# Scores of layer 1 for pairs of heads, in halves of 64 queries, two products side by side in TensorE's columns

## The chip, the cores and the metric

The kernel runs on one core of a Trainium2 chip. The metric is the device time of one execution in microseconds (us), the median of three runs: 2057.37 us before the change (2057.35 to 2057.42). Inside a core, several engines run at the same time and wait for each other through semaphores: TensorE (PE in the profile; its weight loads are shown apart as PEld), VectorE (DVE), ScalarE (ACT), GpSimd (POOL), and SyncE (SP), which only starts transfers.

## The reference

Two transformer layers on x of shape (4, 512, 512). What matters here is the attention of layer 1: 32 query heads and 8 key heads of 128, over 512 tokens, causal, in f32.

```python
q = (hidden_states @ w_q).reshape(B, S, Hkv, g, D)     # 8 key heads, 4 query heads each
k = (hidden_states @ w_k).reshape(B, S, Hkv, D)
v = (hidden_states @ w_v).reshape(B, S, Hkv, D)
scores = jnp.einsum('bqhgd,bkhd->bhgqk', q, k) * scale
causal = jnp.tril(jnp.ones((S, S), dtype=bool))
scores = jnp.where(causal, scores, -jnp.inf)
probs = jax.nn.softmax(scores.astype(jnp.float32), axis=-1).astype(q.dtype)
attn = jnp.einsum('bhgqk,bkhd->bqhgd', probs, v)
return attn.reshape(B, S, Hq * D) @ w_o
```

So the scores of one head are 512 x 512, of which only the lower triangle counts. Query i sees keys 0 to i.

## The kernel before

The whole program is one hand-ordered sequence: each engine executes its instructions in the order in which the code issues them. Layer 0 takes about the first 190 us, the attention of layer 1 runs from there to about 1750 us, and the feed-forward part of layer 1 fills the rest.

The attention of layer 1 is cut into 32 blocks (batch times key head), each with 4 query heads; `score(s, i)` counts the heads through, s = 4n + h. Two heads, a pair, make one `window` (L1120). Window w issues the scores and softmax of pair w+1 and the value products of pair w, and in between it deals out `fill`: the pieces of the q, k, v and output projections (`seven`, L738), each a quarter product of 256 or 128 columns into one of three banks of PSUM from the pool `ps_sc`, and gathered from there by DVE or ACT.

Inside a window the eight score tiles of the pair, `(s, i)` with i the tile of 128 queries, go through a short software pipeline, one step per slot: in slot j the score of tile j (`score`, L872), the division of tile j-1 (`divide`, L889), and the 32 by 32 transposes of tile j-2 (`flip`, L895). The tiles come in the order i = 3, 2, 1, 0 for the first head and then 3, 2, 1, 0 for the second (L1125). In slots 8 and 9 the value products of the pair before follow (`value`, L920), and at the end `carry` (L911) sends the flipped probabilities through transfers that complete the transpose.

For one tile, `score` does this: one product of 128 queries with the first 128(i+1) keys into a bank taken in turn from `ps_mm` and `ps_tr` (L878), an addition of a 128 by 128 mask to the last, diagonal block (L879; the mask holds 0 or -3e38), a maximum over the row (L881), and the exponential with its sum on ACT (L883). The product is f32, and one such product is two instructions of TensorE with a weight load each; the queries are the stationary operand (128 columns of the array), the keys the moving one.

`value` collects a head's output in `av` and copies it on ACT into `oT[n][:, h, :]` (L933). From `oT` POOL makes the left sums of the output projection (`sums_o`, L760), and `o_pieces` (L837) uses them.

The modulation of each layer, in `M` (L386), is of use below as a measuring point: four f32 products of 32 output columns each, placed at columns 0, 32, 64 and 96 of the array (L390).

Of the kernel before, what the change touches and what calls it, by code (L numbers as in the profile page):

```python
# [8 lines left out]
F32 = mybir.dt.float32  # L9
# [4 lines left out]
ALU = mybir.AluOpType  # L14
# [3 lines left out]
P = 128  # L18
# [6 lines left out]
HKV, G, D1 = 8, 4, 128  # L25
INTER = 1792
FB = 256
EPS = 1e-5
NEG = -3.0e38
EXACT = 4096.0  # L30


@with_exitstack
def adaln_two_layers(ctx: ExitStack, tc: tile.TileContext, a, out: bass.AP):
    nc = tc.nc
# [9 lines left out]
    conste = early.enter_context(tc.tile_pool(name="conste", bufs=1))  # L45
    lnp = early.enter_context(tc.tile_pool(name="ln", bufs=1))
    gap = early.enter_context(tc.tile_pool(name="gate_a", bufs=B))
    ps_mm = early.enter_context(tc.tile_pool(name="ps_mm", bufs=2, space=PSUM))
    ps_sc = early.enter_context(tc.tile_pool(name="ps_sc", bufs=3, space=PSUM))
    ps_tr = early.enter_context(tc.tile_pool(name="ps_tr", bufs=2, space=PSUM))  # L50
# [83 lines left out]
    with tc.using_default_side("right"):  # L134
# [15 lines left out]
    nc.vector.memset(mhalf, -0.5)  # L150
    ident = const.tile([P, P], F32, name="ident")
    make_identity(nc, ident)
    mask = conste.tile([P, P], F32, name="mask")
    nc.gpsimd.memset(mask, 0.0)
    nc.gpsimd.affine_select(
        out=mask, in_=mask, compare_op=ALU.is_ge, fill=NEG, base=0,
        pattern=[[-1, P]], channel_multiplier=1,
    )

    o_sb = [l0w.tile([P, NT, 32], F32, name=f"o{b}") for b in range(B)]  # L160
    for b in range(B):
# [3 lines left out]
        cid, pattern=[[0, 1]], base=0, channel_multiplier=1,  # L165
# [54 lines left out]
    ADD, SUB = ALU.add, ALU.subtract  # L220
# [5 lines left out]
    def left_sums(eng, t, s):  # L226

        A11, A21, A12, A22 = quarters(t)
        S3, S2, S4 = s[:, 0], s[:, 1], s[:, 2]
        eng.tensor_tensor(S3, A11, A21, SUB)  # L230
        eng.tensor_tensor(A21, A21, A22, ADD)
        eng.tensor_tensor(S2, A21, A11, SUB)
        eng.tensor_tensor(S4, A12, S2, SUB)
        return {1: A11, 2: A12, 3: S4, 4: A22, 5: A21, 6: S2, 7: S3}
# [15 lines left out]
    def sums_in(kind, n):  # L250
        w = weights[kind, n]
        s = T["wp"].tile([P, 3, 2, w.shape[2] // 2], F32, tag=f"s{kind}", name=f"s{kind}")
        left[kind, n] = left_sums(nc.gpsimd, w, s)
# [455 lines left out]
    for o in order:  # L709
        name, _, eng = o.partition("/")  # L710
# [24 lines left out]
    def bank(shape, name):  # L735
        return ps_sc.tile(shape, F32, tag="sc", name=name)
# [18 lines left out]
    qT, kT, vs, oT, prob = {}, {}, {}, {}, {}  # L755
# [8 lines left out]
    def sums_h(b, engs):  # L764
        s = hp.tile([P, 4, 2, HALF], F32, tag="hT", name="hsum")
        right["h", b] = right_sums(engs, h1[b], [s[:, i] for i in range(3)], s[:, 3])
# [40 lines left out]
    def q_pieces(n):  # L807
        def start():
            for j in range(2):
                qT[n, j] = at.tile([P, 2, S], F32, tag="qT", name="qT", bufs=3)  # L810
            return corners(qT[n, 0], qT[n, 1])

        return seven(lambda: left["q", n], lambda: right["h", n // HKV], gather(start), SEVENTH)
# [37 lines left out]
    BK = 32  # L851
    NG = P // BK
# [13 lines left out]
    def blocks(s, i):  # L866

        if s // 2 == LAST:
            return plain[:, s % 2, i, : (i + 1) * P].rearrange("p (j q) -> p j q", q=BK)
        return prob2[s // 2 % 2][:, : NG * (i + 1), s % 2, i, :]  # L870

    def score(s, i):  # L872
        n, h = divmod(s, G)
        w = (i + 1) * P
        pool, tag = ((ps_mm, "mm"), (ps_tr, "tr"))[i % 2]
        ps = pool.tile([P, 512], F32, tag=tag, name="sc")
        q = qT[n, h // 2][:, h % 2, :]
        nc.tensor.matmul(ps[:, :w], q[:, i * P : w], kT[n][:, :w], start=True, stop=True)  # L878
        nc.vector.tensor_tensor(ps[:, i * P : w], ps[:, i * P : w], mask, ADD)  # L879
        nmx = small.tile([P, 1], F32, tag="nmx", name="nmx")  # L880
        nc.vector.tensor_reduce(nmx, ps[:, :w], AX.X, ALU.max, negate=True)  # L881
        den = small.tile([P, 1], F32, tag="den", name="den")
        nc.scalar.activation(  # L883
            blocks(s, i), ps[:, :w].rearrange("p (j q) -> p j q", q=BK),
            AF.Exp, bias=nmx, accum_out=den,
        )
        prob[s, i] = den

    def divide(s, i):  # L889
        p = blocks(s, i)  # L890
        rden = small.tile([P, 1], F32, tag="rden", name="rden")
        nc.vector.reciprocal(rden, prob.pop((s, i)))  # L892
        nc.scalar.mul(p, p, rden)  # L893
# [17 lines left out]
    def carry(pair):  # L911

        for a_ in range(NG):
            src = prob2[pair % 2][a_ * BK : (a_ + 1) * BK]
            src = src.rearrange("r (k j) h i q -> r j k (h i q)", j=NG)
            for j in range(NG):
                dst = turned[j * BK : (j + 1) * BK, :, a_]
                nc.sync.dma_start(dst, src[:, j])

    def value(s):  # L920

        n, h = divmod(s, G)
        if h == 0:
            oT[n] = at.tile([P, G, S], F32, tag="oT", name="oT")
        av = bank([P, 512], "av") if s % 2 else ps_av.tile([P, 512], F32, tag="av", name="av")
        pT = straight if s // 2 == LAST else turned
        for k in range(NT):
            nc.tensor.matmul(  # L928
                av.rearrange("p (a n) -> p a n", a=NG)[:, :, BK * k :], vs[n][:, k, :],
                pT[:, k, :, P * (s % 2) + BK * k : P * (s % 2 + 1)],  # L930
                start=(k == 0), stop=(k == NT - 1),
            )
        nc.scalar.copy(  # L933
            oT[n][:, h, :].rearrange("p (i a q) -> p a i q", a=NG, q=BK),
            av.rearrange("p (a i q) -> p a i q", a=NG, q=BK),
        )


    def scan(i):
# [122 lines left out]
    def decide():  # L1062
        size = small.tile([P, 1], F32, tag="size", name="size", bufs=1)
        nc.vector.tensor_reduce(size, sizes, AX.X, ALU.max)
        nc.vector.tensor_scalar(size, size, EXACT, None, ALU.is_gt)
        return size
# [9 lines left out]
    def split_pieces(got):  # L1076

        def piece(c):
            if c == 0:
                h2[0] = [hp.tile([P, KC, S], F32R, tag="hT", name=f"h2_{i}") for i in range(2)]  # L1080
            pt, m = bank([P, S], "lnT"), modT[1]
            for t in range(NT):
                nc.tensor.transpose(
                    pt[:, t * P : (t + 1) * P], got["xn"][:, t, c * P : (c + 1) * P], ident
                )

            tag, bufs = (("v", 4), ("kT", 3))[c % 2]
            tm = at.tile([P, E], F32, tag=tag, name="tm", bufs=bufs)
            nc.scalar.activation(
                tm, pt, AF.Identity, bias=m[:, 2, c, 0:1], scale=m[:, 3, c, 0:1]  # L1090
            )
            hi, lo = (h[:, c, :] for h in h2[0])
            nc.scalar.copy(hi, tm)

            lows.append(lambda: nc.vector.tensor_tensor(lo, tm, hi.bitcast(F32), SUB))

        lows = []
        return [lambda c=c: piece(c) for c in range(KC)], [lambda c=c: lows[c]() for c in range(KC)]
# [17 lines left out]
    def run(*fill):  # L1116
        for f in fill:
            f()

    def window(w, fill, side=(), late=(), values=(8, 9)):  # L1120


        fill, side = list(fill), list(side)
        more = w + 1 <= LAST
        tiles = [(2 * w + 2 + h, i) for h in range(2) for i in (3, 2, 1, 0)]  # L1125

        lag, turn_ = (5, turn) if w + 1 == LAST else (2, flip)
        slots = lag + 7
        share = [len(fill) // slots + (i < len(fill) % slots) for i in range(slots)]
        each = -(-len(side) // slots)  # L1130
        for i in range(slots + 1):
            if more and i >= lag:
                turn_(*tiles[i - lag])
            if more and 0 < i < 9:
                divide(*tiles[i - 1])
            if more and i < 8:
                score(*tiles[i])
            for h in range(2):
                if w >= 0 and values[h] == i:
                    value(2 * w + h)  # L1140
            if i < slots:
                for _ in range(share[i]):
                    fill.pop(0)()
                for _ in range(each):
                    if side:
                        side.pop(0)()
        run(*late)
        if w + 1 < LAST:
            carry(w + 1)
# [5 lines left out]
    run(*put(2, x[2]))  # L1155
    sums_h(0, (nc.gpsimd, nc.vector))
    nc.gpsimd.memset(prob2[0], 0.0)
    sums_in("k", 0)
    sums_in("v", 0)
    sums_wo(0)  # L1160
# [9 lines left out]
    run(*put(3, x[3]), *put(0, x[0]), *put(1, x[1]))  # L1170
    q = q_pieces(1)
    window(-1, v_pieces(0))
    load("v", 1)
    pending = []
    begun = []

    for n in range(NBLK):
        b, g = divmod(n, HKV)
        ahead, behind = n + 1 < NBLK, n > 0
        if n > 0:  # L1180
            q = q_pieces(n + 1) if ahead else []
# [3 lines left out]
        kind, m = "vk"[n % 2], n // 2 + n % 2  # L1185
# [40 lines left out]
        else:  # L1226
            first_weights()
            t, r = split_pieces(got)
# [5 lines left out]
            s = at.tile([P, 3, 2, HALF], F32, tag="soT", name="soT", bufs=1)  # L1234
# [262 lines left out]
```

## Time and profile before

The profiled execution took 2058.11 us, of which its span, from the first to the last instruction, is 2056.2 us. The rest lies around the span.

| what | value |
|---|---|
| median of the runs | 2057.37 us |
| profiled execution / span | 2058.11 / 2056.2 us |
| score products L878, duration of one pass of 512, 384, 256, 128 columns | 593, 487, 379, 274 ns |
| weight load of 128 columns for L878 | 191 ns |
| mask on DVE, L879 | 284 ns, 512 times |
| maximum on DVE, L881, 512 / 384 / 256 columns | 692 / 558 / 425 ns |
| exponential on ACT, L883, 512 / 384 / 256 columns | 687 / 581 / 474 ns |
| output copy on ACT, L933 | 581 ns, 128 times |

How to read it: a line of a group names the source line, engine, operation, the tiles written and read, the shapes and how often; then the busy time in us and the mean duration of one in ns; then how long the engine was idle just before and what ended that. In a timeline each row has the start in us, the time in us, the engine, and the instructions merged into the row. A pass of TensorE is shown from its start to the modelled end of its pipeline, so passes in a row overlap in the view; how fast they stream is read from the distance between starts.

### The profile page before, as it was taken

What the parts mean: (1) busy time and instruction counts of PE and PEld (TensorE: products, weight loads), DVE (VectorE), ACT (ScalarE), POOL (GpSimd) and SP (SyncE); (2) the same over time, 40 slices, a digit from 0 to 9 for tenths busy, and PEclk for the clock granted to TensorE, in tenths of its full rate; (3) what the DMA queues carried; (4) which work ended last, traced back from release to release, by engine and by line L of the source; (5) the groups of instructions that cost most, each with busy time, mean ns of one, the idle gap of its engine ahead of it and who ended that gap; (6) DMA issues with size and microseconds to landing.
All of it is one profiled execution on the core that took longest, in us unless ns stands there. A gap on an engine that the chain in (4) does not pass through costs nothing.

```text
span 2056.2 us, 27492 instructions
## 1 busy us (share of the span) xinstructions
PE 2020.9 (98%) x9219; PEld 1580.4 (77%) x9219; DVE 1362.9 (66%) x3323; ACT 878.9 (43%) x1998; POOL 756.9 (37%) x656
## 2 busy tenths in 40 slices
PE   6999999999999999999999999999999999999998
PEld 4655777878787887877787878787877777888887
DVE  6766776677667666766677676667666674655554
ACT  3421554445444444544444445444444454223322
POOL 2314234434336443353473334337333333800000
PEclk8799999999999999999999999999999999999999
DMA  8310656676657766655766665567656556600000
GB/s 299 123 62 30 173 151 175 159 175 153 144 144 192 180 160 161 164 144 152 186 182 163 154 164 133 144 154 177 167 144 154 141 128 202 196 21 1 21 21 22
DMA packets 243640, 288.59 MB, mean 140 GB/s; under 512 B 23250, under 2 KB 184018, under 8 KB 243492
## 3 DMA queue, kind: packets, MB, share of 16 engines
q1 hardware_dynamic: 242964, 285.71, 52.8%
q8 instruction: 76, 1.25, 0.3%
q10 hardware_dynamic: 528, 1.05, 0.2%
q14 instruction: 72, 0.59, 0.1%
HBM read 142.99 MB, written 11.57 MB: 75 GB/s over the span
## 4 chain that ended last, share of the span: by engine, by line
PE 94%; DVE 3%; ACT 1%; issue 1%; DMA 1%; POOL 0%; SPq 0%; DVEq 0%; ACTq 0%
PE quarter L746 46%; PE av L928 14%; PE sc L878 13%; PE p_gate L1347 5%; PE p_up L1347 5%; PE acc L1366 4%; PE ffn L634 2%; PE lnT L477 1%; PE modps L390 1%; PE lg L593 1%; PE qkv_ps L507 1%; PE modT_ps L403 1%; PE add_ps L578 1%; DVE bnst L60 0%; DMA c_sb<-in_L_cT_dram 0%
## 5 line engine op out<-in xcount | busy, mean ns | idle before, releaser
L878 PE MATMUL sc<-kT,qT 128*128 128x512 f32 (+3 forms) x1024 | 355.1, 433 | 0.0
L928 PE MATMUL av<-x,v 128*128 128x512 f32 x1008 | 295.7, 437 | 3.7 <-DMA x<-p 3.7
L928 PEld LDWEIGHTS av<-x,v 128*128 128x128 f32 x1008 | 190.3, 192 | 110.7 <-issue 66.5
L881 DVE TENSOR_REDUCE nmx<-sc 128x1 f32<-128x512 f32 (+3 forms) x512 | 251.6, 491 | 17.7
L893 ACT ACTIVATE x<-x,rden 128x512 f32<-128x512 f32 (+3 forms) x256 | 143.6, 561 | 235.4 <-DVE rden L892 235.4
L778 DVE TENSOR_TENSOR qT<-qT,quarter 128x512 f32<-128x512 f32 x224 | 150.5, 684 | 133.9 <-PE quarter L746 127.7
L893 ACT ACTIVATE p<-p,rden 128x512 f32<-128x512 f32 (+3 forms) x256 | 143.7, 561 | 221.5 <-DVE rden L892 219.8
L879 DVE TENSOR_TENSOR sc<-sc,mask 128x128 f32<-128x128 f32 x512 | 145.5, 284 | 136.5 <-PE sc L878 135.6
L842 DVE TENSOR_TENSOR acc<-acc,quarter 128x512 f32<-128x512 f32 x196 | 134.5, 686 | 134.6 <-PE quarter L746 134.4
L230 POOL TENSOR_TENSOR sq<-wq 128x512 f32<-128x512 f32 x32 | 40.6, 1269 | 471.5 <-DMA wq<-in_L_attn_w_q_dram 453.0
L878 PEld LDWEIGHTS sc<-kT,qT 128*128 128x128 f32 x1024 | 182.6, 191 | 24.2
L746 PEld LDWEIGHTS quarter<-wo,oT 128*128 128x128 f32 x744 | 140.9, 190 | 43.9 <-issue 20.1
L746 PE MATMUL quarter<-wo,oT 128*128 128x256 f32 x744 | 171.1, 379 | 0.2 <-ACT oT L933 0.2
L883 ACT ACTIVATE p<-sc,nmx 128x512 f32<-128x512 f32 (+3 forms) x256 | 135.1, 528 | 75.8 <-DVE nmx L881 67.1
L883 ACT ACTIVATE x<-sc,nmx 128x512 f32<-128x512 f32 (+3 forms) x256 | 134.9, 527 | 70.1 <-DVE nmx L881 65.4
L933 ACT COPY oT<-av 128x512 f32<-128x512 f32 x128 | 74.3, 581 | 167.0 <-PE av L928 165.0
L896 DVE STREAM_TRANSPOSE p<-p 128x512 f32<-128x512 f32 (+3 forms) x256 | 129.4, 506 | 2.0 <-ACT p L893 0.5
L896 DVE STREAM_TRANSPOSE x<-x 128x512 f32<-128x512 f32 x248 | 125.0, 504 | 1.3 <-ACT x L893 0.9
L746 PE MATMUL quarter<-hsum,sq 128*128 128x256 f32 x512 | 121.1, 379 | 1.4 <-DVE hsum L244 1.4
L746 PEld LDWEIGHTS quarter<-hT,wq 128*128 128x128 f32 x512 | 97.2, 190 | 32.4 <-issue 14.8
L746 PE MATMUL quarter<-hsum,wq 128*128 128x256 f32 x512 | 121.0, 379 | 0.0
L746 PE MATMUL quarter<-hT,wq 128*128 128x256 f32 x512 | 120.9, 379 | 0.0
(257 smaller groups left out, 3752.7 us busy)
## 6 DMA issues: line engine op xcount, KB each, us to landing
x<-p SPq DMA_DIRECT2D x512, 128.0 KB, 3.7
x<-x SPq DMA_DIRECT2D x496, 128.0 KB, 3.8
wq<-in_L_attn_w_q_dram SPq DMA_DIRECT2D x32, 1024.0 KB, 5.6
wo<-in_L_attn_w_o_dram SPq DMA_DIRECT2D x31, 1024.0 KB, 5.7
wm<-in_L_wmod_dram SPq DMA_DIRECT2D x12, 1024.0 KB, 9.6
wk<-in_L_attn_w_k_dram SPq DMA_DIRECT2D x16, 512.0 KB, 3.7
wv<-in_L_attn_w_v_dram SPq DMA_DIRECT2D x16, 512.0 KB, 3.8
xn<-x_d SPq DMA_DIRECT2D x28, 256.0 KB, 5.9
```

The costliest lines, as they stand in the source:

```text
L746: nc.tensor.matmul(ps[:, m, :], l[:, k, m * P : (m + 1) * P], r[:, k, :], start=(k == 0), stop=(k == 1),)
L778: nc.vector.tensor_tensor(c[out], c[v], ps, ADD if sign > 0 else SUB)
L842: nc.vector.tensor_tensor(osum[:, i - 1], osum[:, i - 1], ps, ADD)
L878: nc.tensor.matmul(ps[:, :w], q[:, i * P : w], kT[n][:, :w], start=True, stop=True)
L879: nc.vector.tensor_tensor(ps[:, i * P : w], ps[:, i * P : w], mask, ADD)
L881: nc.vector.tensor_reduce(nmx, ps[:, :w], AX.X, ALU.max, negate=True)
L883: nc.scalar.activation(blocks(s, i), ps[:, :w].rearrange("p (j q) -> p j q", q=BK), AF.Exp, bias=nmx, accum_out=den,)
L893: nc.scalar.mul(p, p, rden)
L896: nc.vector.transpose(blocks(s, i), blocks(s, i))
L928: nc.tensor.matmul(av.rearrange("p (a n) -> p a n", a=NG)[:, :, BK * k :], vs[n][:, k, :], pT[:, k, :, P * (s % 2) + BK * k : P * (s % 2 + ...
L1347: nc.tensor.matmul(ps[kind], w[kind][:, k, c * P : (c + 1) * P], h2[b % 2][i][:, k, :], start=(k == 0 and i == 0), stop=(k == KC - 1 and i ...
L1366: nc.tensor.matmul(acc[t], act[i][:, t * P : (t + 1) * P], w[:, c, :], start=(n == 0 and i == 0), stop=(n == NI - 1 and i == 1),)
```

## The change

A pair's scores for tile i are now issued together, by the first head's `score`, as four products of 64 queries each: first half and second half of the 128 queries, for each of the two heads. The first half leaves out the last 64 keys, which lie above the diagonal for all its queries. Two products of the same half, one for each head, go to the two 64-column halves of the array and so to the two halves of the partitions of two different banks. For the first head the first half of the queries lies in partitions 0 to 63; for the second head it lies in partitions 64 to 127, with the halves exchanged.

What follows from that: there are two masks, the second with its halves exchanged; the mask is applied by a minimum, so that what stands in the columns that are no longer computed is covered too; four fixed banks `sc_ps` from `ps_mm` and `ps_tr` replace the tiles taken in turn, and are set to 0 once; the tiles of a window come in the order i = 3, 2, 1, 0 with both heads of each i in succession; and the second head's output copy becomes two copies, which put the exchanged halves back.

```diff
+TOP = 3.4028234e38
...
-    mask = conste.tile([P, P], F32, name="mask")
-    nc.gpsimd.memset(mask, 0.0)
-    nc.gpsimd.affine_select(
-        out=mask, in_=mask, compare_op=ALU.is_ge, fill=NEG, base=0,
-        pattern=[[-1, P]], channel_multiplier=1,
-    )
+    masks = conste.tile([P, 2, P], F32, name="masks")
+    nc.gpsimd.memset(masks, TOP)
+    HP = P // 2
+    for m, ps_, first_ in ((0, slice(0, P), 0), (1, slice(0, HP), HP), (1, slice(HP, P), 0)):
+        nc.gpsimd.affine_select(
+            out=masks[ps_, m], in_=masks[ps_, m], compare_op=ALU.is_ge, fill=NEG, base=first_,
+            pattern=[[-1, P]], channel_multiplier=1,
+        )
...
+    sc_ps = [[p.tile([P, 512], F32, tag=t, name="sc") for _ in range(2)] for p, t in ((ps_mm, "mm"), (ps_tr, "tr"))]
+
+    def product(s, i):
+        n, h = divmod(s, G)
+        for half in range(2):
+            w = i * P + HP * (half + 1)
+            for h_ in range(2):
+                q = qT[n, (h + h_) // 2][:, (h + h_) % 2, :]
+                at_ = HP * (half ^ h_)
+                nc.tensor.matmul(
+                    sc_ps[h_][i % 2][at_ : at_ + HP, :w], q[:, w - HP : w], kT[n][:, :w],
+                    start=True, stop=True, tile_position=(0, at_),
+                )
+
     def score(s, i):
-        n, h = divmod(s, G)
-        w = (i + 1) * P
-        pool, tag = ((ps_mm, "mm"), (ps_tr, "tr"))[i % 2]
-        ps = pool.tile([P, 512], F32, tag=tag, name="sc")
-        q = qT[n, h // 2][:, h % 2, :]
-        nc.tensor.matmul(ps[:, :w], q[:, i * P : w], kT[n][:, :w], start=True, stop=True)
-        nc.vector.tensor_tensor(ps[:, i * P : w], ps[:, i * P : w], mask, ADD)
+        if s % 2 == 0:
+            product(s, i)
+        w, ps = (i + 1) * P, sc_ps[s % 2][i % 2]
+
+        nc.vector.tensor_tensor(ps[:, i * P : w], ps[:, i * P : w], masks[:, s % 2], ALU.min)
...
-        nc.scalar.copy(
-            oT[n][:, h, :].rearrange("p (i a q) -> p a i q", a=NG, q=BK),
-            av.rearrange("p (a i q) -> p a i q", a=NG, q=BK),
-        )
+        dst = oT[n][:, h, :].rearrange("p (i a q) -> p a i q", a=NG, q=BK)
+        src = av.rearrange("p (a i q) -> p a i q", a=NG, q=BK)
+        if h % 2 == 0:
+            nc.scalar.copy(dst, src)
+        else:
+            nc.scalar.copy(dst[:, 2:], src[:, :2])
+            nc.scalar.copy(dst[:, :2], src[:, 2:])
...
-        tiles = [(2 * w + 2 + h, i) for h in range(2) for i in (3, 2, 1, 0)]
+        tiles = [(2 * w + 2 + h, i) for i in (3, 2, 1, 0) for h in range(2)]
...
     nc.gpsimd.memset(prob2[0], 0.0)
+    for ps in sc_ps[0] + sc_ps[1]:
+        nc.vector.memset(ps, 0.0)
```

## The prediction

> **What bounds the kernel now.** I read the page from the top: busy times, the chain that ended last, then who waited on TensorE.
>
> ```profile
> span 2056.2 us, 27492 instructions
> PE 2020.9 (98%) x9219; PEld 1580.4 (77%) x9219; DVE 1362.9 (66%) x3323; ACT 878.9 (43%) x1998; POOL 756.9 (37%) x656
> ...
> PE 94%; DVE 3%; ACT 1%; issue 1%; DMA 1%; POOL 0%; SPq 0%; DVEq 0%; ACTq 0%
> PE quarter L746 46%; PE av L928 14%; PE sc L878 13%; PE p_gate L1347 5%; PE p_up L1347 5%; PE acc L1366 4%; PE ffn L634 2%; PE lnT L477 1%; PE modps L390 1%; PE lg L593 1%; PE qkv_ps L507 1%; PE modT_ps L403 1%; PE add_ps L578 1%; DVE bnst L60 0%; DMA c_sb<-in_L_cT_dram 0%
> ```
>
> TensorE is the chain, and the scores (L878) are 13% of it. The list of waits, for PE alone, says that nothing in the attention holds TensorE up:
>
> ```profile
> PE modps L390 <- DMA wm<-in_L_wmod_dram: 11.9, 1, 11.9
> PE modT_ps L403 <- DVE part L286: 4.3, 3, 2.0
> PE av L928 <- DMA x<-p: 3.7, 1, 3.7
> ```
>
> So a nanosecond more or less of TensorE time in the attention is a nanosecond of the end. The groups by form show the score products that are to change, and the one f32 product of the kernel that already runs in column tiles (modps, four tiles of 32 columns):
>
> ```profile
> L878 PE MATMUL sc<-kT,qT 128*128 128x512 f32 x256 | 130.9, 593 | 0.0
> L878 PE MATMUL sc<-kT,qT 128*128 128x384 f32 x256 | 103.6, 487 | 0.0
> L878 PE MATMUL sc<-kT,qT 128*128 128x256 f32 x256 | 76.2, 379 | 0.0
> L878 PE MATMUL sc<-kT,qT 128*128 128x128 f32 x256 | 49.3, 274 | 0.0
> ```
>
> Each f32 product is two instructions (x256 for 128 products). A duration holds the pipeline's latency too; throughput is the distance between starts. In the timeline of PE at 809 us, 14 passes of 256 columns take 3.19 us; less one latency-bearing pass of 0.38, that is 2.81/13 = 0.216 us for a pass, 0.84 ns a column, 1.68 ns a column for both passes. Check: 64 pairs of heads x 2 x (128+256+384+512) columns x 1.68 ns = 275 us, against 12.9% of 2056 = 265 us in the chain.
>
> **What the skill says, and whether the trace agrees.** "TensorEngine Tiling (Array Packing)", Key Properties, says that changing the tiling mode, not just the tile, drains TensorE, and that different tiles run in parallel. "TensorE: Matmul & The Clock Gate", Part 3, gives 2.38x for three column tiles of 512 columns. The trace has both, in f32, in the PE timeline around one modps group:
>
> ```profile
> 34.21 0.93 PE L477 MATMUL lnT<-ident,xn 128*128 128x128 f32 x7
> 35.06 1.06 PE L390 MATMUL modps<-wm,silu_c 128*32 128x512 f32 x8
> 36.06 0.42 PE L507 MATMUL qkv_ps<-wcat,h1n 128*128 128x48 f32 x2
> ```
>
> Eight passes of 512 columns end to end would take 8 x 0.43 = 3.4 us; they take 1.06 with the latency, two rounds of four side by side. So tiles do overlap. But the seven transposes start 0.108 us apart, the last at 34.86, and are streamed by 34.97; the group begins at 35.06, 0.09 later. At its end likewise: two rounds from 35.06 are streamed by 35.97 (0.91 us, of which 2 x 0.43 is streaming and some 0.03 the first weights), and qkv begins at 36.06. In the attention itself one product of another width stands between ordinary ones:
>
> ```profile
> 1291.24 0.81 PE L746 MATMUL quarter<-wo,oT 128*128 128x256 f32 x3
> 1291.98 0.19 PE L1070 MATMUL wide_ps<-ones,size 128*1 128x1 f32 x2
> 1292.10 0.91 PE L878 MATMUL sc<-kT,qT 128*128 128x384 f32 x2
> 1292.85 0.38 PE L746 MATMUL quarter<-so,oT 128*128 128x256 f32 x1
> ```
>
> The third quarter pass starts at 1291.67 and is streamed 0.215 later, at 1291.89; the next starts 0.09 after that. The score product behind it lasts from 1292.10 to 1292.85 before the next starts: 0.75, where 384 columns x 1.68 ns are 0.645. The missing 0.105 is the weight load, which a drain leaves uncovered; the same view of the groups in a window around it gives this first pass 590 ns, against the 487 of its form above. "LDWEIGHTS" in the same TensorE page prices it by columns, P/1.2 ns: 107 for 128, 53 for 64, 27 for 32. The trace agrees at both ends it has (0.105 for 128; some 0.025 to 0.03 for modps' 32); 64 it doesn't show.
>
> **The change, part by part.**
>
> 1. Columns saved. Before, a pair of heads streams 2 x 128(i+1) columns for query tile i. After, the first halves of both heads run side by side over 128i+64 columns, the second halves over 128i+128: 256i+192. That is 64 columns less for each i, 256 a pair: 256 x 1.68 ns x 64 pairs = 27.5 us off TensorE, if the two tiles overlap fully.
>
> 2. Mode changes. The order of TensorE's instructions puts the four products of one (pair, i) together, with 128-column work before and after every one: 256 groups, 512 changes. Into the group: drain 0.094, and the load of 64 columns in the open, 0.053 (an estimate from the page's price and the two ends measured; bounds 0 and 0.105). Out of it: drain 0.094 and the load of 128 columns, 0.105. What follows is nearly always a quarter product of 256 columns, whose pass (0.215) covers its own next load, so nothing is hidden twice. Sum 0.346 x 256 = 88.6 us. Nothing covers it: TensorE is the chain.
>
> 3. Softmax ends. The mask becomes a minimum of the same shape (284 ns a piece, as now): nothing. The order 3,3,2,2,1,1,0,0 instead of 3,2,1,0 twice puts wide reductions first: 2 x 0.69 + 2 x 0.56 against 0.69+0.56+0.43+0.29 in the first four steps, 0.53 us more on DVE, given back in the last four. Three banks of quarters (1.7 us each) lie between DVE and TensorE, and DVE idles for some 2 us twice at a window's end (its timeline at 804 and 807 us): taken at 0. With that cover gone it costs at most 0.53 x 63 windows = 33 us. A product now waits until both heads' exponentials of the bank's earlier use are done, but that score stands three steps, some 8 us, back; all of TensorE's queue is behind the wait, should it come late: 0, within the same 33.
>
> 4. Output copies. 64 copies of 581 ns become two of half the columns. The exponentials give 687-474 = 213 ns for 256 columns, so two copies take some 2 x 368 = 736: 64 x 0.155 = 10 us more on ACT, which is 43% busy; TensorE waited on such a copy for 0.2 us in all. The left sums on POOL and the output products behind them start 0.16 later and have a window of over 20 us to spare: 0; bounded by those 10 us.
>
> 5. Start. POOL's two further selects and larger memset (0.35 and 0.2 each before) lie ahead of 10.9 us of idling: 0. Four DVE memsets of a bank, priced by the nearest 128x512 row (0.69), are 2.8 us at 192 us, in front of the first gathers; three banks hide most: I take 1, bounds 0 and 2.8.
>
> No DMA is added or moved, and SP's queue keeps its order.
>
> Sum against the profiled execution (2058.11 us with what lies around its span, 0.7 above the median 2057.37): -27.5 + 88.6 + 1 = +62, so 2120 us, the same to the microsecond against either.
>
> **The rivals.**
>
> - Faster: the sequencer loads the weights of both modes ahead, so that a change costs next to nothing when it comes in a full stream. The place is the boundary of each group; it decides from 27.5/256 = 107 ns for both changes together. Then 2058 - 27.5 + 1 = 2032. Against it: every change of width in the trace shows the 0.09, even in the full stream at 1291.98, and two drains alone (188) pass the 107.
> - Only the drains count, the loads hide under them: 256 x 0.188 = 48, less 27.5: 2079. Against it: the 590 ns pass.
> - The tiles overlap only in part. The order within a group is tile 0, 1, 1, 0, and each product has two passes. "TensorE: Matmul & The Clock Gate", Part 3, says that products start in strict program order; if both passes of a product go out before the next tile's, tile 0's second pass overlaps tile 1's first, and a group takes three rounds where I count two: 1.5 x 2304 = 3456 columns a pair instead of 2560 before, +96 us, with the changes +185: 2244. Against it: modps' first four passes start together, so passes of different tiles are interleaved there.
> - DVE's burst stalls TensorE in each window: up to 33 us more, 2153. DVE's idle tail speaks against it.
>
> **How the numbers follow.** Forecast 0.80; only drains 0.05; partial overlap 0.05; burst 0.03; faster 0.07. Range of the forecast: the entry's load from 0 to 0.105 is -13.6 to +13.3 us; a share of points 3 to 5 may add 10 more; and some of the load could hide on the way out. 2095 to 2145. What a measurement of this kernel can tell from no change is about 0.2% (4 us); no case lies there, so I leave 0.01 for same; slower 0.92, faster 0.07.
>
> **What would show it.** In the profile after: L888 score passes of 64 columns, two starting within some 10 ns; 0.09 us between the end of streaming before and the first load, and again after; a first quarter pass of some 480 ns instead of 379 after each group; a TensorE with idle time before the weight loads, put down to "issue"; DVE and ACT with longer waits on PE. Wrong if quarter passes follow a group without that gap, if paired passes start a whole pass apart, or if TensorE waits on DVE in each window.

## The result, and the profile after

The changed kernel takes 2119.01 us (median; 2117.95 to 2119.91), the kernel before 2057.39 in the same comparison: a ratio of 1.0299, 95% interval 1.0281 to 1.0317. The profiled execution took 2117.95 us, 59.8 more than that of before. The page of the changed kernel, its head and its chain of waits:

```profile
span 2116.2 us, 30145 instructions
PE 2080.0 (98%) x10243; PEld 1512.7 (71%) x10243; DVE 1363.0 (64%) x3327; ACT 878.3 (42%) x2062; POOL 756.1 (36%) x658
...
PE 91%; DVE 4%; ACT 1%; SPq 1%; DMA 1%; issue 1%; POOL 1%; ACTq 0%; DVEq 0%
PE quarter L750 45%; PE av L947 13%; PE sc L888 13%; PE p_gate L1371 5%; PE p_up L1371 5%; PE acc L1390 4%; PE ffn L638 2%; PE lnT L481 1%; SPq L937 1%; PE lg L597 1%; PE modps L394 1%; PE qkv_ps L511 1%; DVE nmx L900 1%; DMA x<-p 1%; PE add_ps L582 0%
```

TensorE is still the chain, and the 98% hide the loss: a pass that starts together with its weight load counts as busy from there on, though it streams later. What shows the loss is the timeline of PE around one group of score products (i = 3), 803 us into the execution:

```profile
801.97 1.14 PE L947 MATMUL av<-x,v 128*128 128x384 f32 x5
803.04 1.83 PE L888 MATMUL sc<-kT,qT 128*64 128x448 f32 x8
804.80 0.71 PE L750 MATMUL quarter<-wv,hsum 128*128 128x128 f32 x4
```

and that of the weight loads in the same stretch; in brackets the idle time before a load:

```profile
802.72 0.19 PEld L947 LDWEIGHTS av<-x,v 128*128 128x128 f32 x1
803.03 0.20 PEld L888 LDWEIGHTS sc<-kT,qT 128*64 128x64 f32 x4
803.46 0.14 PEld L888 LDWEIGHTS sc<-kT,qT 128*64 128x64 f32 x2 [0.23 <-issue]
803.84 0.14 PEld L888 LDWEIGHTS sc<-kT,qT 128*64 128x64 f32 x2 [0.23 <-issue]
804.79 0.63 PEld L750 LDWEIGHTS quarter<-wv,hsum 128*128 128x128 f32 x5 [0.81 <-issue]
```

Read together: the last value pass starts at 802.83 and is streamed after 0.107; the first score load starts at 803.03, 0.096 later. The second pair of passes follows the first after 0.43 us, where 448 columns stream in 0.373: the load of 64 columns lay in the open for 0.053. No weights for the quarter product are loaded during the group, although PEld was idle for 0.81 us: they start at 804.79, 0.094 after the last score pass was streamed. And in the trace the second quarter pass starts 0.213 after the first, where 0.112 is the step of a row of such passes. Over all 256 groups the medians are 95 ns into the group, 54 for the open load, 94 out of it, and 107 for the second open load. (A pass counts as streamed after 0.833 ns a column: passes of 512 columns in a row start 429 ns apart and those of 256 columns 216, and 213 for 256 columns is 0.833 for one.) Where a quarter product of 256 columns follows, in 201 of the 256 groups, its first pass takes 483 ns by the median, for the 480 that the prediction named as a sign.

The two tiles do work side by side. The timeline narrowed to 803.02 to 803.05 us shows the row before and the first two passes, which start in that window, 6 ns apart, one in each tile:

```profile
802.83 0.28 PE L947 MATMUL av<-x,v 128*128 128x128 f32 x1
803.04 0.60 PE L888 MATMUL sc<-kT,qT 128*64 128x448 f32 x2
```

Of the 2048 score passes 2022 have such a partner, which starts within 30 ns.

One more thing is new, in the list of waits of PE:

```profile
PE sc L888 <- ACT x L902: 4.5, 4, 1.3
```

Four times, about 1.1 us each, a score product waits for an exponential. No wait of that kind was in the list before.

### The profile page after: what moved, and what is told of

Same layout as the page of the kernel before. It is cut to its first block, busy times and chain, and to the rows that moved or that the text cites. A ratio compares the mean times of both kernels' runs of the same rounds, so it can differ in the third digit from the quotient of the medians.

```text
span 2116.2 us, 30145 instructions
## 1 busy us (share of the span) xinstructions
PE 2080.0 (98%) x10243; PEld 1512.7 (71%) x10243; DVE 1363.0 (64%) x3327; ACT 878.3 (42%) x2062; POOL 756.1 (36%) x658
## 4 chain that ended last, share of the span: by engine, by line
PE 91%; DVE 4%; ACT 1%; SPq 1%; DMA 1%; issue 1%; POOL 1%; ACTq 0%; DVEq 0%
PE quarter L750 45%; PE av L947 13%; PE sc L888 13%; PE p_gate L1371 5%; PE p_up L1371 5%; PE acc L1390 4%; PE ffn L638 2%; PE lnT L481 1%; SPq L937 1%; PE lg L597 1%; PE modps L394 1%; PE qkv_ps L511 1%; DVE nmx L900 1%; DMA x<-p 1%; PE add_ps L582 0%
## 5 line engine op out<-in xcount | busy, mean ns | idle before, releaser
L888 PE MATMUL sc<-kT,qT 128*64 128x448 f32 (+7 forms) x2048 | 307.9, 419 | 4.5 <-ACT x L902 4.5
L898 DVE TENSOR_TENSOR sc<-sc,masks 128x128 f32<-128x128 f32 x512 | 144.7, 283 | 197.1 <-PE sc L888 197.1
L888 PEld LDWEIGHTS sc<-kT,qT 128*64 128x64 f32 x2048 | 114.5, 136 | 117.7 <-issue 70.9
L750 PE MATMUL quarter<-wo,oT 128*128 128x256 f32 x744 | 177.1, 387 | 0.3 <-ACT oT L958 0.3
L750 PEld LDWEIGHTS quarter<-wo,oT 128*128 128x128 f32 x744 | 136.2, 190 | 51.5 <-issue 25.5
L915 DVE STREAM_TRANSPOSE x<-x 128x512 f32<-128x512 f32 (+1 forms) x248 | 124.9, 504 | 1.2 <-ACT x L912 0.9
L750 PE MATMUL quarter<-so,soT 128*128 128x256 f32 x496 | 120.4, 386 | 0.0
## 6 DMA issues: line engine op xcount, KB each, us to landing
wm<-in_L_wmod_dram SPq DMA_DIRECT2D x12, 1024.0 KB, 10.5
```

The source lines that it names most:

```text
L750: nc.tensor.matmul(ps[:, m, :], l[:, k, m * P : (m + 1) * P], r[:, k, :], start=(k == 0), stop=(k == 1),)
L888: nc.tensor.matmul(sc_ps[h_][i % 2][at_ : at_ + HP, :w], q[:, w - HP : w], kT[n][:, :w], start=True, stop=True, tile_position=(0, at_),)
L915: nc.vector.transpose(blocks(s, i), blocks(s, i))
```

## The experiments

The theory, A: a group of 64-column products costs its two mode changes, two drains and two weight loads in the open, and everything else comes to next to nothing. Rival B: the slow-down comes from what was changed around the products, the order of the tiles, the waits for both heads and the double copies. Rival C: it goes with the number of small products, not with the groups. There were two series, each with its own runs of the kernel before on the same chip: 2056.67 us for the full products, the columns not saved, the two query tiles and the first form of the saving without column tiles; 2057.68 for the other three.

**The products made full again.**

```diff
     def product(s, i):
         n, h = divmod(s, G)
-        for half in range(2):
-            w = i * P + HP * (half + 1)
-            for h_ in range(2):
-                q = qT[n, (h + h_) // 2][:, (h + h_) % 2, :]
-                at_ = HP * (half ^ h_)
-                nc.tensor.matmul(
-                    sc_ps[h_][i % 2][at_ : at_ + HP, :w], q[:, w - HP : w], kT[n][:, :w],
-                    start=True, stop=True, tile_position=(0, at_),
-                )
+        w = (i + 1) * P
+        for h_ in range(2):
+            q = qT[n, (h + h_) // 2][:, (h + h_) % 2, :]
+            nc.tensor.matmul(
+                sc_ps[h_][i % 2][:, :w], q[:, i * P : w], kT[n][:, :w],
+                start=True, stop=True,
+            )
...
-        nc.vector.tensor_tensor(ps[:, i * P : w], ps[:, i * P : w], masks[:, s % 2], ALU.min)
+        nc.vector.tensor_tensor(ps[:, i * P : w], ps[:, i * P : w], masks[:, 0], ALU.min)
...
-            nc.scalar.copy(dst[:, 2:], src[:, :2])
-            nc.scalar.copy(dst[:, :2], src[:, 2:])
+            nc.scalar.copy(dst[:, 2:], src[:, 2:])
+            nc.scalar.copy(dst[:, :2], src[:, :2])
```

No halves are exchanged any more, so both heads take the first mask, and the two copies keep the halves in place.

> The order of the tiles, the minimum with a mask, the four fixed banks, the memsets and the double copy of the second head stay as in the changed kernel; the products are of 128 queries over all 128(i+1) keys again, one a head, both issued together. Theory A (mode changes cost 0.346 us a group, everything else next to nothing): no change of width is left and the columns are those of before, so 2057 to 2060 us. Rival B (the slow-down comes from the new order, the waits for both heads' exponentials and the copies): it stays near 2119 - 27 + 27 = 2119, or at least above 2080.

Measured: 2062.72 us, 6.0 above the kernel before; ratio 1.0029 (1.0020 to 1.0039). So nearly all of the slow-down goes with the products' form, and B falls as the main cause. But six microseconds are left, three more than A allows, and its list of waits has the same line as above:

```profile
PE sc L886 <- ACT x L900: 5.0, 4, 1.3
```

**The columns not saved.** The first halves run over all 128(i+1) keys too; all else is the changed kernel.

```diff
-            w = i * P + HP * (half + 1)
+            w, lo = (i + 1) * P, i * P + HP * half
...
-                    sc_ps[h_][i % 2][at_ : at_ + HP, :w], q[:, w - HP : w], kT[n][:, :w],
+                    sc_ps[h_][i % 2][at_ : at_ + HP, :w], q[:, lo : lo + HP], kT[n][:, :w],
```

> The changed kernel, but the first halves run over all 128(i+1) keys as well, so the columns that TensorE streams are those of before, and the groups stay 256. Theory A: the 27.5 us of saved columns go, 2119 + 27.5 = 2146 us, 89 above the kernel before. If tiles overlapped only in part, the difference to the changed kernel would be 41 us (three rounds of 64 columns for two), 2160.

Measured: 2145.46 us, ratio 1.0447 (1.0418 to 1.0475), so 88.8 above the kernel before and, by the medians' differences to before, 27.2 above the changed kernel's 61.6. (One of the four runs took 2155.61; by the ratios it would be 30.) That is the saving of the columns at full overlap rather than the 41 of a partial one, and the passes that start in pairs in the trace say the same. And against the run with full products, which streams the same columns in the same order, 82.7 us are the price of the column tiles alone, with whatever waits they lengthen or shorten: 0.323 us for each of 256 groups.

**Two query tiles in one group.**

```diff
-        if s % 2 == 0:
-            product(s, i)
+        if s % 2 == 0 and i % 2:
+            product(s, i)
+            product(s, i - 1)
```

> The products of two query tiles, i = 3 and 2 or 1 and 0, are issued together, so that 128 groups are left of 256 and nothing else is taken away. Theory A: half of 88.6 us goes, 2119 - 44 = 2075 us. Rival B: the waits come earlier and are longer, 2119 or more. Rival C (the cost goes with the number of small products, not of groups): 2119.

Measured: 2220.12 us, ratio 1.0795 (1.0777 to 1.0813): 101 us slower than the changed kernel where A says 44 faster. The list of waits of PE tells why the time of this run can't decide between A and the rest:

```profile
PE sc L888 <- ACT x L903: 79.0, 61, 3.2
PE sc L888 <- ACT p L903: 16.8, 18, 1.7
```

The product of i = 0 goes to the banks of i = 2, whose exponentials were issued a step or two before; now it stands at once behind them, and all of TensorE's queue stands behind it. These 96 us are the wait for banks that the prediction named in its point 3 and took at 0, brought about here by the experiment itself. The price of the groups did fall by half: in the trace the drains and open loads of the 128 groups sum to 43 us, those of the changed kernel's 256 to 89 (places that took over 0.2 us, by a wait or a lower clock, are left out). There is a second loss, in the table of stretches (busy time of each engine, then PE's granted clock), here 478 to 490 us of this run:

```profile
478.00:490.00 12.00, 6.44 (x28) 4.45 (x27) 7.24 (x22) 5.04 (x11) 1.45 (x2) 0.66 0.36 85
```

and the same stretch of the changed kernel:

```profile
478.00:490.00 12.00, 12.00 (x62) 8.33 (x61) 6.95 (x16) 3.56 (x9) 5.09 (x4) 1.00 0.93 227
```

The clock is half from 481.8 to 492.0 us, from within the first of two waits, of 2.55 and 3.01 us, until 6 us after the second. The rows of PE show it: eight passes of 256 columns take 3.78 us, and 1.89 when the clock is full again.

```profile
482.26 0.48 PE L888 MATMUL sc<-kT,qT 128*64 128x64 f32 x2 [2.55 <-ACT x L903]
485.75 0.91 PE L888 MATMUL sc<-kT,qT 128*64 128x64 f32 x6 [3.01 <-ACT x L903]
486.58 3.78 PE L750 MATMUL quarter<-hT,wq 128*128 128x256 f32 x8
...
492.80 1.89 PE L750 MATMUL quarter<-hT,sq 128*128 128x256 f32 x8
```

Over the whole span the mean clock is 0.973 against 0.989, which is 2218.1 x 0.027 - 2116.2 x 0.011 = 37 us of full clock more lost, part of it while TensorE would have waited anyway. With -44 + 96 and up to 37 that makes up to 89 of the 101 us. Some 9 of the rest are passes that the waits tore apart, as the first two rows show: 258 of the 2048 score passes have no partner that starts within 30 ns, against 26 in the changed kernel, and by streaming alone they add 10.6 us against 1.9.

**Only the first two tiles in one group.** The clean form of the same question: i = 3 and 2 go together, where the banks have long been free.

```diff
-        if s % 2 == 0:
-            product(s, i)
+        if s % 2 == 0 and i != 2:
+            product(s, i)
+            if i == 3:
+                product(s, 2)
```

> The changed kernel, with only the products of i = 3 and i = 2 issued together; their banks were last used by i = 1 and 0 of the pair before, with value products in between, so the waits that spoiled the run with both twos together shouldn't be there. 192 groups of 256 are left. Theory A (a group costs its two mode changes, some 0.34 us less the boundary that stays): 64 x 0.34 = 22 us less than the changed kernel, 2097 us. Rival C (the cost goes with the number of small products): 2119.

Measured: 2110.68 us (2108.02 to 2119.66), ratio 1.0245 (1.0215 to 1.0276), some 8 to 11 us faster than the changed kernel by medians and ratios, at most half of what A says. The profiled execution is the slowest of the five, 2119.66 us: against the changed kernel's it lost 11 us before the attention, where its clock was half for one stretch of 58 us and the changed kernel's for 34. From the first to the last score pass it took 10.7 us less than the changed kernel, and for this part the trace gives the rest. The drains and open loads of 192 groups sum to 66.4 us where those of 256 in the changed kernel sum to 89.0 (places of over 0.2 us left out), so the 22 did go. But the places where TensorE stood for more than 0.15 us after the end of streaming, at full clock, sum to 18.8 us (22 of them) against 8.9 (6); the list of waits has new lines, of which these are the largest:

```profile
PE quarter L750 <- DVE ve L1035: 2.9, 4, 0.8
PE quarter L750 <- DVE v L782: 1.5, 3, 0.5
```

C is out as the whole cause, since the number of small products is the same and the time is not; the price that A puts on a group holds, and about half of the gain is given back in waits on DVE and ACT, which A had at next to nothing.

**The columns saved without column tiles.** Both heads of a pair have the same keys. So 64 queries of the one and 64 of the other can be one ordinary stationary operand of 128 columns, and the first halves still leave out their last 64 keys.

```diff
-                qT[n, j] = at.tile([P, 2, S], F32, tag="qT", name="qT", bufs=3)
+                qT[n, j] = at.tile([P, 2 * S], F32, tag="qT", name="qT", bufs=3)
...
-        n, h = divmod(s, G)
-        w = (i + 1) * P
+        n, h = divmod(s - s % 2, G)
+        w = i * P + HP * (s % 2 + 1)
+        if s // 2 == LAST and s % 2 == 0:
+            nc.gpsimd.memset(plain[:, 0, i, w : w + HP], 0.0)
...
-        q = qT[n, h // 2][:, h % 2, :]
-        nc.tensor.matmul(ps[:, :w], q[:, i * P : w], kT[n][:, :w], start=True, stop=True)
-        nc.vector.tensor_tensor(ps[:, i * P : w], ps[:, i * P : w], mask, ADD)
+        q = qT[n, h // 2][:, 2 * (w - HP) : 2 * w]
+        nc.tensor.matmul(ps[:, :w], q, kT[n][:, :w], start=True, stop=True)
+        nc.vector.tensor_tensor(ps[:, w - HP : w], ps[:, w - HP : w], mask, ADD)
...
+            heads = pT[:, k, 2 * (s % 2) : 2 * (s % 2) + 2, :].rearrange("p a (t n) -> p t a n", t=2)
             nc.tensor.matmul(
-                av.rearrange("p (a n) -> p a n", a=NG)[:, :, BK * k :], vs[n][:, k, :],
-                pT[:, k, :, P * (s % 2) + BK * k : P * (s % 2 + 1)],
+                av.rearrange("p (t a n) -> p t a n", t=2, a=2)[:, :, :, BK * k :], vs[n][:, k, :],
+                heads[:, :, :, BK * k :],
```

Left out here: the mask of 64 columns for both halves, the views through which the queries are laid out in blocks of 64 by head, and zeros for the probabilities that are no longer computed.

> The columns are saved without column tiles: the kernel before, with 64 queries of the first head and 64 of the second as one stationary operand of 128 columns (both heads have the same keys), first halves without their last 64 keys. The queries are laid out in blocks of 64 by head for it, the softmax works on tiles of both heads and is 64 columns narrower for the first halves, and the value product picks its head's blocks of 32 by the moving operand's pattern. Theory A: only the 27.5 us of saved columns remain, 2057 - 27.5 = 2030 us. If the narrower products didn't pay off on TensorE, because something else came to bound the windows: 2057. If the patterns with three free dimensions or the strided queries slowed their instructions: above 2057.

Measured: 2044.66 us, ratio 0.9949 (0.9933 to 0.9964): faster than the kernel before, but by 12 us, not 27. The first line of its waits of PE is new:

```profile
PE pT L917 <- POOL x L885: 15.9, 1, 15.9
```

In the last pair a few blocks must be set to 0, and I had put that on POOL, where it stood behind sums that waited 5.05 us for a late transfer, and behind casts of weights. One edit moves it:

```diff
-            nc.gpsimd.memset(plain[:, 0, i, w : w + HP], 0.0)
+            nc.vector.memset(plain[:, 0, i, w : w + HP], 0.0)
```

> The stacked kernel with its four small memsets for the last pair on DVE in place of POOL, where they stood behind the weights' conversions and held TensorE for 16 us. Theory A: those 16 us go and the columns' 27.5 us are left as the whole difference to the kernel before, 2028 to 2030 us. If the stall was waiting time that something else would have needed anyway: 2040 or more.

Measured: 2030.37 us (2029.30 to 2031.14), ratio 0.9863 (0.9834 to 0.9892), 27.3 below the kernel before in the same comparison, for 27.5 counted. The forms of its score products show where it comes from: eight widths, of the ordinary 128 columns of the array, at the durations of the kernel before where the widths are the same; here the widest two of them and the narrowest:

```profile
L889 PE MATMUL sc<-kT,qT 128*128 128x512 f32 x128 | 65.5, 593 | 0.0
L889 PE MATMUL sc<-kT,qT 128*128 128x448 f32 x128 | 58.7, 540 | 0.0
...
L889 PE MATMUL sc<-kT,qT 128*128 128x64 f32 x128 | 21.2, 248 | 0.0
```

In the changed kernel the form of 448 columns takes 565 on average, since every other one of its passes starts with an open load:

```profile
L888 PE MATMUL sc<-kT,qT 128*64 128x448 f32 x256 | 63.1, 565 | 0.0
```

That the total agrees to 0.2 us is in part chance. Behind the narrowest of these products TensorE's next pass mostly starts 112 ns after its second one, where 53 of streaming and some 3 would be 56: the load of 128 columns that follows takes 107 and is not covered. That is 3.5 us more than counted for 63 such places. On the other side the longest wait of the value product, 3.7 us for a transfer in the trace of the kernel before, is 0.9 here.

**Whose product waits.** The six microseconds left by the first experiment: its kernel, with each head's product issued by its own score.

```diff
-        for h_ in range(2):
-            q = qT[n, (h + h_) // 2][:, (h + h_) % 2, :]
+        for h_ in (s % 2,):
+            q = qT[n, h // 2][:, h % 2, :]
...
-        if s % 2 == 0:
-            product(s, i)
+        product(s, i)
```

> The run with full products, but each head's product is issued by its own score again, not both by the first head's; the order of the tiles, the fixed banks, the minimum, the memsets and the double copy stay. That run was 6 us slower than the kernel before. If the six come from a product's wait for both heads' exponentials and from two products at once, they go: 2057 us. If they come from the order of the tiles, the copies or the memsets, they stay: 2062 us.

Measured: 2057.08 us, ratio 0.9995 (0.9982 to 1.0007). The six are gone, and so is the line of the score waiting for ACT; the list of waits of PE begins:

```profile
PE modps L394 <- DMA wm<-in_L_wmod_dram: 12.4, 1, 12.4
PE modT_ps L407 <- DVE part L290: 3.8, 3, 2.0
PE av L944 <- DMA x<-p: 3.4, 1, 3.4
```

So the order of the tiles, the minimum, the fixed banks, the memsets and the double copies cost nothing that can be seen, and the joint issue costs six.

## Why the prediction was right

The forecast was 2120 us, the result 2119.01. What carried it is right: the price of the mode changes is the slow-down, and the saved columns are small beside it. That the two agree within 1 us is luck, since two errors of some 6 and 5 us cancel. Its terms, one by one:

1. Columns saved, 27.5 us: the run without the saving puts it at 27.2. The tiles overlap fully, so the rival of partial overlap (2244) is out. The trace shows the first passes of both tiles together and then the second passes, as modps had shown; whether the program or TensorE puts them in this order, no run here tells.

2. Mode changes, 88.6 us: the pair of runs with the same columns puts them at 82.7. The trace has 95 + 54 + 94 + 107 = 350 ns for a group, for 346 forecast; so the load of 64 columns, for which the formula under "LDWEIGHTS" in the Trainium skill's "TensorE: Matmul & The Clock Gate" gives 53 and which was estimated from two other widths, was right, and the drain that the skill's "TensorEngine Tiling (Array Packing)", Key Properties, names without a price is 0.094 to 0.095 in each direction. What the forecast left out: a boundary without a change also has some 2.7 ns at each of the four places, so 350 - 11 = 339 ns or 87 us are the difference. Another 3 us are waits that were shorter (places of over 0.15 us, counted as above from the first to the last score pass, sum to 7.4 us in the run with all columns and to 10.5 in the run with full products), probably since TensorE came later to them. The last 1 us is less than medians of these runs scatter by.

3. What stood in points 3 to 5 was taken at 1 us and came to 6.0, by the run with full products. The step that failed is the wait for both heads' exponentials, taken at 0 because "that score stands three steps, some 8 us, back". The distance is right: the products of i = 2 start at 460.59 us in the window looked at here, those of i = 0 at 468.40. But in four windows it is not enough. In the timeline of the changed kernel at 468 us:

```profile
466.58 1.89 PE L750 MATMUL quarter<-hsum,wq 128*128 128x256 f32 x8
468.40 0.33 PE L888 MATMUL sc<-kT,qT 128*64 128x64 f32 x2
469.78 0.55 PE L888 MATMUL sc<-kT,qT 128*64 128x64 f32 x6 [1.05 <-ACT x L902]
```

The first head's tile starts, the second head's waits 1 us for its own bank. Before, that product was issued by its own score, a step later. DVE shows what makes the bank late in this window:

```profile
467.34 0.16 DVE L1039 SCALAR_TENSOR_TENSOR nmr<-bnmv,rstd 128x4 f32<-128x4 f32 x1 [1.13 <-POOL rstd L1035]
...
468.40 0.56 DVE L900 TENSOR_REDUCE nmx<-sc 128x1 f32<-128x384 f32 x1
```

The last row is the maximum of the second head's tile i = 2, without which its exponential can't start. Ahead of it in DVE's queue stands a layer norm, in which DVE waits 1.13 us for POOL. All four windows have this: L1035 starts at 466.3, 865.7, 1264.8 and 1714.0 us, and the waits of TensorE end at 469.8, 869.2, 1268.3 and 1717.4. No run moved the layer norm away, so that it is the cause is read from the order alone. The effect was named and its upper end of 33 us kept; the value taken was too low by 5. It made up for most of what the mode changes cost less.

The other parts were as worked out: two copies of half the columns take 378 and 372 ns (736 counted for both), and TensorE waits for them 0.3 us in all, where it was 0.2; the four memsets take 2.11 us (2.8 counted as the bound) and show in no wait of TensorE.

The faster rival asked for two changes in under 107 ns; two drains alone are 189. The rival "only the drains" (2079) is out by the open loads. The burst of DVE that would stall TensorE in every window did not come about: the four windows above are all.

## What to carry to other kernels

A stretch of column tiles has to save more than its two edges cost: here each stretch of 0.3 to 2 us lost 0.34 us at its edges, against 0.107 saved, and the break-even could be counted beforehand from places in the old trace where the tile width changes. By that count modps is such a stretch, eight passes in 1.06 us where 3.4 would be end to end; the groups of scores are not. Before splitting the array, look for operands that can be put side by side in one ordinary stationary operand: two heads with the same keys gave the saving without those edges, 2030 us. And when products are issued ahead in pairs, every buffer of the pair must be free at the first one's place in the queue, so the wait moves forward too.

## What the runs showed of the hardware that was not expected

In the run with two query tiles in a group, waits of TensorE well under 3 us were at times followed by a lower clock, so that stalled time was paid for a second time after the stall. Between 200 and 1860 us of that run the clock is half in 16 stretches of 3.4 to 10.2 us. Four of them come with waits of 2.5 to 3.2 us, as the one at 482 us does; the other twelve follow a wait of 1.5 to 1.8 us, most of them with a shorter one just before it. Of some 28 waits of this length not even half were followed by a lower clock; what decides, no run here tells. In the changed kernel, whose groups each have two breaks of 0.1 us and two open loads, the clock is full from 184 to 1764 us, and its four waits of 1.0 to 1.3 us for ACT did not change that. The Trainium skill's "TensorE: Matmul & The Clock Gate", in the table under "Why this matters for your kernels", puts the limit at idle gaps of some 3 us between bursts of products; here the clock fell at times after gaps of little more than half of that, and the measurement decides.
